# Order statistics in a four-layer graph kernel: z rows by transfers, k and table differences on ScalarE, and the last layers in layer 0's buffers

## The chip, the cores and the metric

The kernel runs on one core of one Trainium2 chip. The metric is the time of one execution on the device in microseconds (us); the kernel before took 14073.2 us (median of three runs, 14069.84 to 14090.67).

## The reference, cut to what matters

There are 16 batch elements of 1024 nodes with 64 channels, and one 1024 x 1024 adjacency matrix each. Four layers follow one another, each of the form `x = x + layer(relu(layernorm(x)), adj)`.

```python
# layer 0: thin the adjacency, then for each node and channel three quantiles over its neighbours
adj_d = _dilate_adj(adj, mask)
sv = jnp.sort(where(valid, x, big)); m = valid.sum(-1)
for tau, wt in zip([.25, .5, .75], [.25, .5, .25]):
    pos = clip(tau * (m - 1), 0); lo = floor(pos); hi = ceil(pos)
    agg += wt * (gather(lo) * (1 - frac) + gather(hi) * frac)
h = relu((x + agg) @ W1 + b1); y = (h @ W2 + b2) * mask
# layer 1: (A + I) x / rowsum        layer 2: attention, 8 heads of 64, softmax(g0*q k^T + g1*adj)
# layer 3: adj @ (x W3) + b3
```

Layer 0 is an order-statistic problem: for each node, channel and six positions k (floor and ceil of three quantiles), the k-th smallest value among the node's neighbours.

## The kernel before, in words

**Layer 0.** The channels of an element are sorted once (`ranks`, a bitonic network on VectorE), and the neighbours are thinned (`dilate`). Then `picks` walks 1536 steps: 16 elements x 8 groups of 8 channels x 2 halves of 512 nodes x 6 positions q. Before the six steps of a (group, half), `group` (L668) counts with matmuls how many neighbours of a node lie below each block of sorted values: `cum` (L694, copied from PSUM by ScalarE) holds the counts, `c0` and `c1` hold packed words. A step then compares `cum` with row `krow[q]` (`le`, L735), masks the two words with it (`wa`, `wb`, L737 and L739), reduces them with matmuls (L751), finds the place within the block (`bits`, L766 to L772) and the value (`value`, L779). After the sixth q of a (group, half), `value` adds the six results (`agg`, L785), weights them (`w`, L794), folds them with the matmul `acc` (L797) into eight rows of a 64-row PSUM tile whose other rows are zero, and VectorE adds (for group 0, copies) all 64 rows to `el.z` (L804, L802). `el.z` is [128, 2, 512]: for each half, 64 rows of h and 64 rows of sums. `leave` (L954) multiplies `z` by W1 twice (`ph`, L962), then by W2, adds to x and gives the element to the later layers.

**What an element needs first.** `stages` (L923) prepares the next element in the last steps of the present one: the neighbour tile, the counts `m1` (L588), six rows `krow` (L602, L603: multiply and add, then shift right, in integers on VectorE; L605: cast to fp16 by ScalarE), and `sorted_table` (L621), whose differences `df` are multiplied out of PSUM by VectorE (L639, four per element). Sorting and thinning of the next element (`background`) are given out one piece per step.

**Layers 1 to 3.** `rest(b)` runs layer 1, layer 2 and layer 3 of an element. The main loop at the end pays it out against the steps: a step is worth 0.42 units, a row block of layer 2 costs 1.0. So the layers of element b run among the steps of element b + 1, and those of the last element run alone after the last step. In layer 2, for each of four pairs of heads (`pr`), k, q and v are made (L1045, L1057), and for each of eight row blocks i: a row block `ad` of the adjacency is loaded (L420, three buffers) and scaled by ScalarE; the scores of two 512-column halves go to one PSUM tile `sp` with one buffer (L1074); VectorE adds `ad` and takes the minimum (L1083); ScalarE takes the exponent of the two heads (`s`, two buffers of tag b4) ; TensorE transposes it through `pcols` (L412), ScalarE copies it to `eT` (L415, two buffers of tag bt), and TensorE multiplies it with v (`ao`, L1093) and the projection (`pp`, L1104).

**What sets the order.** Each engine works its own instructions in one order, fixed when the kernel is built, as does SyncE's queue, from which all transfers are issued. Waits between engines are semaphores. A buffer of a ring (`a2` has four, `b4`, `pa`, `pb`, `pc` two each) is free again when its last reader is done, a transfer included.

**Start.** L130 to L145 make a table of bit-reversed numbers, [128, 1024] with equal rows, by ten rounds of two VectorE operations, and write it to DRAM; `ranks` reads it back (L528) eight times in all.

Of the kernel before, what the change touches and what calls it, by code (L numbers as in the profile page):

```python
# [29 lines left out]
TOP = 2.0 ** 23  # L30
MID = 1600.0
UP = 4096.0
LOW = 2048.0


@with_exitstack
def tile_preln_adj_stack(
# [57 lines left out]
    def a2(name, shape=(P, 512), dt=F32):  # L95
        return sb.tile(list(shape), dt, tag="a2", bufs=4, name=name)
# [5 lines left out]
        return ps.tile(list(shape), dt, tag="pc", bufs=2, name=name)  # L102


    def b4(name, shape=(P, N), dt=F32):
        return sb.tile(list(shape), dt, tag="b4", bufs=2, name=name)

    def pb(name, shape=(P, 512), dt=F32):
        return ps.tile(list(shape), dt, tag="pb", bufs=2, name=name)

    def small(name, shape, dt=F32, bufs=3):
# [6 lines left out]
    def sc(name, shape=(P, P), dt=F32):  # L118
        return scrp.tile(list(shape), dt, name=name)
# [7 lines left out]
    identh = const.tile([P, P], HP, name="identh")  # L127
    nc.vector.tensor_copy(identh, identf)

    rev_i = sc("rev_i", (P, N), I32)  # L130
    nc.gpsimd.iota(rev_i, pattern=[[1, N]], base=0, channel_multiplier=0)
    rev_a = sc("rev_a", (P, N), I32)
    rev_b = sc("rev_b", (P, N), I32)
    nc.vector.memset(rev_a, 0)
    for b_ in range(N.bit_length() - 1):
        up = N.bit_length() - 2 - 2 * b_
# [2 lines left out]
            op1=OP.logical_shift_left if up >= 0 else OP.logical_shift_right,  # L139
        )  # L140
        nc.vector.tensor_tensor(rev_a, rev_a, rev_b, OP.bitwise_or)
    rev = sc("rev", (P, N), HP)
    nc.vector.tensor_copy(rev, rev_a)
    rev_d = dram.tile([P, N], HP, name="rev_d")
    nc.sync.dma_start(rev_d, rev)  # L145
    not_i = const.tile([P, P], BF, name="not_i")
    nc.vector.tensor_scalar(not_i, identf, -1.0, 1.0, op0=OP.mult, op1=OP.add)
# [23 lines left out]
    par = const.tile([P, 2], F32, name="par")  # L171
    nc.vector.tensor_copy(par[:, 1:2], par_i[:, 0:1])
    nc.vector.tensor_scalar(par[:, 0:1], par[:, 1:2], -1.0, 1.0, op0=OP.mult, op1=OP.add)
    for c2 in range(2):
        cols = slice(c2 * BKW, (c2 + 1) * BKW)
        for i, w in enumerate((1.0, LOW)):
            nc.vector.tensor_scalar(
                sel_w[:, i, cols], fcol_i[:, :BKW], 0.0, w, op0=OP.mult, op1=OP.add
            )
            nc.vector.tensor_scalar(sel_w[:, i, cols], sel_w[:, i, cols], par[:, c2 : c2 + 1], None, op0=OP.mult)  # L180
# [44 lines left out]
    for i in range(2):  # L225
        nc.vector.tensor_tensor(sel_t[:, i, 8 * i : 8 * i + 8], pblk[:, 0:8], fcol_i[:, 0:8], OP.is_equal)

    sel_c = const.tile([P, 2 * (D - 8) + 8], F32, name="sel_c")
    nc.vector.memset(sel_c, 0.0)
    nc.vector.tensor_scalar(pblk, prow_i, 7, None, op0=OP.bitwise_and)  # L230
    nc.vector.tensor_tensor(sel_c[:, D - 8 : D], pblk[:, 0:8], fcol_i[:, 0:8], OP.is_equal)


    tab_d = const.tile([P, 2, P], F32, name="tab_d")
# [27 lines left out]
    nc.vector.memset(mid_c[:, 0:1], MID)  # L262
    nc.vector.memset(mid_c[:, 1:2], MID * LOW)
    nc.vector.memset(mid_c[:, 2:3], -MID)

    sel_q = const.tile([P, NQ, 2 * BKW], BF, name="sel_q")
    for q in range(NQ):
# [93 lines left out]
    def act(out_, in_, func=AF.Copy, **kw):  # L361
        nc.scalar.activation(out_, in_, func, **kw)  # L362
# [42 lines left out]

    def chunk_cols(ad, name):

        aT = sb.tile([P, C, P], F32, tag="bt", bufs=2, name=name)
        for s in range(2):
            pt = pb("pcols", (P, 4, P))  # L410
            adjoining(
                nc.tensor.transpose(pt[:, c, :], ad[:, (4 * s + c) * P : (4 * s + c + 1) * P], identf)  # L412
                for c in range(4)
            )
            nc.scalar.copy(aT[:, 4 * s : 4 * s + 4, :], pt)  # L415
        return aT
# [65 lines left out]
    def ranks(V):  # L482
# [42 lines left out]
        nc.sync.dma_start(vs, F)  # L525
        yield "half"
        R = b2_("rev", (P, N), HP)
        nc.sync.dma_start(R, rev_d)  # L528

        last = (len(steps) - 1) // 4  # L530

# [51 lines left out]
    def positions(valid):  # L583

        m1 = sb.tile([P, N], I16, tag="m1", bufs=1, name="m1")  # L588
        for t in range(NH):
            pm = pa("pm")  # L590
            adjoining(
                nc.tensor.matmul(
                    pm, ones, valid[:, j, t * 512 : (t + 1) * 512], start=j == 0, stop=j == C - 1
                )
                for j in range(C)
            )
            nc.vector.tensor_scalar(m1[:, t * 512 : (t + 1) * 512], pm, -1.0, None, op0=OP.add)
        yield None
        krow = []
        for q in range(NQ):  # L600
            n = a2("n", (P, N), I16)
            nc.vector.tensor_scalar(n, m1, q // 2 + 1.0, 3.0 * (q % 2), op0=OP.mult, op1=OP.add)  # L602
            nc.vector.tensor_scalar(n, n, 2, None, op0=OP.logical_shift_right)  # L603
            krow.append(sb.tile([P, N], HP, tag="krow", bufs=NQ, name="krow"))
            nc.scalar.copy(krow[q], n)  # L605
            if q < NQ - 1:
                yield None
        n6 = a2("n6", (P, N), I16)
        nc.vector.tensor_scalar(n6, m1, q_tau, q_add, op0=OP.mult, op1=OP.add)
        nc.vector.tensor_scalar(n6, n6, 2, None, op0=OP.logical_shift_right)  # L610
        kq = sb.tile([P, N], HP, tag="kq", bufs=1, name="kq")
        nc.scalar.copy(kq, n6)
        yield krow, kq
        nr = a2("nr", (P, N), I16)
        nc.vector.tensor_scalar(nr, m1, r_tau, None, op0=OP.mult)
        nc.vector.tensor_scalar(nr, nr, 3, None, op0=OP.bitwise_and)
        coef = sb.tile([P, N], BF, tag="coef", bufs=1, name="coef")
        nc.vector.tensor_scalar(coef, nr, w_frac, w_one, op0=OP.mult, op1=OP.add)
        yield coef

    def sorted_table(s, vs):  # L621

        rows = slice(s * D, (s + 1) * D)
        u = q4("u", (P, 8, D))
        pt = pa("put", (P, 8, D))  # L630
        for q in range(8):
            nc.tensor.transpose(pt[:, q, :], vs[rows, q * P : (q + 1) * P], identf[rows, rows])
        nc.scalar.copy(u, pt)
        df = q4("df", (P, D // 2, 2, 8, 2))
        for e in range(2):
            pd = pa("pd", (P, 8, D // 2, 2))
            nc.tensor.matmul(pd, tab_d[:, e, :], u, start=True, stop=True)
            for c2 in range(2):
                nc.vector.tensor_scalar(  # L639
                    df[:, :, c2, :, e], pd[:, :, :, c2].rearrange("p q c -> p c q"),  # L640
                    par[:, c2 : c2 + 1], UP, op0=OP.mult, op1=OP.mult,
                )
        yield None
        tab = sb.tile([P, 2, D // 2, 2 * BKW], HP, tag="tab", bufs=1, name="tab")
        df = df.rearrange("p c s q e -> p (c s q e)")
        for i in range(2):
            part = tab[:, i].rearrange("p c k -> p (c k)")
            nc.vector.tensor_copy(part, df)
            if i < 1:
                nc.vector.tensor_tensor(df, df, part, OP.subtract)  # L650
        yield tab
# [16 lines left out]
    def group(g, t, bk, pw, valid, weights):  # L668
# [16 lines left out]
        for pp in range(4):  # L685
# [5 lines left out]
                nc.tensor.matmul(pc, cw[:, j, :], valid[:, j, hs], start=j == 0, stop=j == C - 1)  # L691
                for j in range(C)
            )
            nc.scalar.copy(cum[:, pp, :], pc)  # L694
            if late is not None:
                low_part(*late)
            pw_ = pc_("pword")
# [15 lines left out]
    def picks():  # L713
# [61 lines left out]
        def value(n):  # L775
# [5 lines left out]
            if q < NQ - 1:  # L781
# [10 lines left out]
            hs = slice(t * 512, (t + 1) * 512)  # L792
            w = a2("w")
            nc.vector.tensor_tensor(w, agg, el.coef[:, hs], OP.mult)  # L794
            half = slice(t * D, (t + 1) * D)
            acc = pb("acc")
            nc.tensor.matmul(  # L797
                acc[half, :], sel_c[:, D - 8 - 8 * g : 2 * D - 8 - 8 * g], w,
                start=True, stop=True, tile_position=(0, t * D), skip_group_check=True,
            )  # L800
            if g == 0:
                nc.vector.tensor_copy(el.z[half, t, :], acc[half, :])  # L802
            else:
                nc.vector.tensor_tensor(el.z[half, t, :], el.z[half, t, :], acc[half, :], OP.add)  # L804

        els[0] = arrive(0)
        for r in background(0):
# [209 lines left out]
    def layer2(b, xr):  # L1017
# [17 lines left out]
        HW = H * D  # L1035
        for pr in range(H // 2):

            kT = sb.tile([P, N], F32, tag="kT", bufs=1, name="kT")
            qT = sb.tile([P, N], F32, tag="qT", bufs=1, name="qT")
            v = sb.tile([P, C, P], F32, tag="v2", bufs=1, name="v2")  # L1040
            for t in range(NH):
                hs = slice(t * 512, (t + 1) * 512)
                both = ((kT, slice(0, D), pb("pk")), (qT, slice(D, P), pb("pq")))
# [19 lines left out]
            for i in range(C):  # L1063
# [5 lines left out]
                nms = [None, None]  # L1069
                for t in range(NH):  # L1070
                    hs = slice(t * 512, (t + 1) * 512)
                    sps = ps.tile([P, 2, 512], F32, tag="sp", bufs=1, name="sp")
                    adjoining(
                        nc.tensor.matmul(  # L1074
                            sps[:, e, :], qT[e * D : (e + 1) * D, i * P : (i + 1) * P],
                            kT[e * D : (e + 1) * D, hs], start=True, stop=True,
                        )
                        for e in range(2)
                    )
                    for e in range(2):  # L1080

                        nm = small("nm", [P, 1], bufs=6)
                        nc.vector.tensor_tensor_reduce(  # L1083
                            ss[e][:, hs], sps[:, e, :], ad[:, hs], -1.0, 3.0e38 if t == 0 else nms[e],
                            op0=OP.add, op1=OP.min, accum_out=nm,
                        )
                        nms[e] = nm
# [61 lines left out]
    for r in picks():  # L1149
        due += r  # L1150
        while due > 0.0:
            due -= next(two) or due
    for _ in two:
        pass

# [33 lines left out]
```

## Time and profile before

| | |
|---|---|
| median of three runs | 14073.2 us |
| the profiled execution | 14083.12 us |
| its span, first to last instruction | 14080.9 us |
| granted TensorE clock, mean | 0.978 |
| start: until the first compare (L735) | 348 us |
| 1536 steps | 348 to about 13621 us |
| last element's layers 1 to 3 alone | about 13621 to 14081 us |
| VectorE busy | 12849.4 us (91%) |
| TensorE busy (matmuls) | 12452.1 us (88%) |
| ScalarE busy | 8198.1 us (58%) |
| the transfers' share of the 16 DMA engines | 18.8% |

The execution that was profiled took 2.2 us more than its span and 9.9 us more than the median. In a line of the profile, "x" gives how often a group of instructions ran; after the bar stand busy us and the mean ns of one; then the idle time of the engine just ahead of them, and who ended it. A line number can be that of a helper (L362 is the call of every ScalarE activation). GpSimd does next to nothing here.

### The profile page before, as it was taken

How to read it: one execution, taken by the hardware profiler on the slowest of the kernel's cores; microseconds unless marked ns; L12 is line 12 of the kernel's file. 1: busy time of each engine (PE TensorE's matmuls, PEld its weight loads, DVE VectorE, ACT ScalarE, POOL GpSimd, SP SyncE). 2: the span in 40 equal slices, each digit the busy share in tenths (PEclk: the TensorE clock that was granted, in tenths of full speed). 3: DMA queues.
4: the chain of work that ended last, by engine and by line, in shares of the span. 5: the costliest groups of instructions: out<-in, count | busy, mean ns of one | idle time of the engine just before them, and what ended most of it. 6: DMA issues, size and time to landing. Idle time of an engine off the chain costs nothing. (4 is left out here: it accounts for less than half of the span.)

```text
span 14080.9 us, 236134 instructions
## 1 busy us (share of the span) xinstructions
PE 12452.1 (88%) x94402; PEld 5955.5 (42%) x95489; DVE 12849.4 (91%) x23280; ACT 8198.1 (58%) x14170; POOL 25.0 (0%) x138
## 2 busy tenths in 40 slices
PE   1889989999899998999899998998989999999987
PEld 0224444444444444444444444444444444444444
DVE  9999999999999999999999999999989999988863
ACT  1446656566566665656566665665656566665655
POOL 0000000000000000000000000000000000000000
PEclk9999999999999999999999999999999999999999
DMA  3012121211212112121211212122121211202011
GB/s 95 28 35 65 47 82 49 77 55 51 77 47 84 49 55 71 53 79 50 70 57 55 76 49 78 49 66 66 48 76 50 71 61 53 82 25 62 26 58 55
DMA packets 478672, 838.40 MB, mean 60 GB/s; under 512 B 232448, under 2 KB 234624, under 8 KB 477568
## 3 DMA queue, kind: packets, MB, share of 16 engines
q1 hardware_dynamic: 477568, 823.24, 18.8%
q8 instruction: 747, 12.24, 0.4%
q14 instruction: 357, 2.92, 0.1%
HBM read 616.27 MB, written 206.83 MB: 58 GB/s over the span
## 5 line engine op out<-in xcount | busy, mean ns | idle before, releaser
L699 PE MATMUL pword<-valid,dw 128*128 128x512 fp8e4 x8192 | 1985.5, 385 | 141.6 <-DVE dw L665 101.3
L691 PE MATMUL pc<-valid,cw 128*128 128x512 fp8e4 x8192 | 1973.9, 381 | 26.0 <-DVE valid L479 13.9
L737 DVE TENSOR_TENSOR wa<-le,c 128x2048 f16<-128x2048 f16 x1536 | 1865.8, 1215 | 134.8 <-PE prep L751 119.6
L735 DVE TENSOR_TENSOR le<-cum,krow 128x2048 f16<-128x2048 f16 x1536 | 1863.6, 1213 | 16.5 <-PE val L751 16.4
L739 DVE TENSOR_TENSOR wb<-le,c 128x2048 f16<-128x2048 f16 x1536 | 1864.1, 1214 | 3.5 <-PE prep L751 3.3
L362 ACT ACTIVATE s<-s,nm 128x1024 f32<-128x1024 f32 x1024 | 1169.9, 1143 | 728.3 <-DVE nm L1083 727.0
L758 ACT COPY wi<-prep 128x512 f32<-128x512 f32 x1536 | 896.8, 584 | 943.3 <-PE prep L751 796.9
L362 ACT ACTIVATE hi<-pword,mid_c 128x512 f16<-128x512 f32 x1024 | 703.2, 687 | 1140.4 <-PE pword L704 1135.5
L1074 PE MATMUL sp<-kT,qT 64*128 64x512 f32 x4096 | 1168.8, 646 | 200.8 <-DVE nm L1083 192.5
L699 PEld LDWEIGHTS <-dw 128*128 128x128 bf16 x8192 | 763.5, 99 | 1262.6 <-DVE dw L665 228.0
L412 PE MATMUL pcols<-identf,s 128*128 128x128 f32 x8192 | 1156.1, 283 | 155.7 <-ACT s L362 74.7
L691 PEld LDWEIGHTS <-cw 128*128 128x128 bf16 x8192 | 764.5, 98 | 1085.4 <-issue 250.1
L412 PEld LDWEIGHTS pcols<-identf,s 128*128 128x128 f32 x8192 | 913.8, 143 | 627.1 <-ACT eT L415 238.8
L415 ACT COPY eT<-pcols 128x512 f32<-128x512 f32 x2048 | 1110.1, 593 | 85.2 <-PE pcols L412 83.3
L1093 PE MATMUL ao<-eT,v 128*64 128x128 f32 x16384 | 1079.9, 277 | 63.8 <-ACT eT L415 60.7
L751 PE MATMUL val<-le,tab 128*32 128x512 f16 x12288 | 1092.2, 388 | 47.7 <-DVE vs L779 30.4
L779 DVE SCALAR_TENSOR_TENSOR vs<-pz,vs 128x512 f32<-128x512 f32 x1536 | 1045.0, 680 | 65.4 <-PE pv L1057 14.9
L362 ACT ACTIVATE vs<-val 128x512 f32<-128x512 f32 x1536 | 927.1, 604 | 235.7 <-PE val L751 146.3
L1093 PEld LDWEIGHTS ao<-eT,v 128*64 128x64 f32 x16384 | 905.5, 137 | 317.3 <-ACT eT L415 212.6
L694 ACT CAST cum<-pc 128x512 f16<-128x512 f32 x1024 | 603.8, 590 | 719.0 <-PE pc L691 674.7
L751 PE MATMUL prep<-wb,sel_w 128*32 128x512 f16 x6144 | 642.5, 396 | 261.8 <-DVE wb L739 238.5
L362 ACT ACTIVATE c<-pword,mid_c 128x512 f16<-128x512 f32 x1024 | 711.2, 695 | 196.9 <-PE pword L681 182.7
(260 smaller groups left out, 19147.0 us busy)
## 6 DMA issues: line engine op xcount, KB each, us to landing
ad<-in_adj_dram SPq DMA_DIRECT2D x768, 512.0 KB, 3.6
adjT_d<-aT SPq DMA_DIRECT2D x128, 512.0 KB, 4.6
aT<-adjT_d SPq DMA_DIRECT2D x128, 512.0 KB, 3.7
md<-sm SPq DMA_DIRECT2D x216, 256.0 KB, 2.0
sb<-md SPq DMA_DIRECT2D x216, 256.0 KB, 2.9
rem_d<-rem SPq DMA_DIRECT2D x128, 256.0 KB, 2.0
left_d<-left SPq DMA_DIRECT2D x128, 256.0 KB, 2.6
left<-left_d SPq DMA_DIRECT2D x128, 256.0 KB, 3.8
```

Of the source, the lines that this page charges most:

```text
L362: nc.scalar.activation(out_, in_, func, **kw)
L412: nc.tensor.transpose(pt[:, c, :], ad[:, (4 * s + c) * P : (4 * s + c + 1) * P], identf)
L415: nc.scalar.copy(aT[:, 4 * s : 4 * s + 4, :], pt)
L691: nc.tensor.matmul(pc, cw[:, j, :], valid[:, j, hs], start=j == 0, stop=j == C - 1)
L699: nc.tensor.matmul(pw_, dw[:, j, :], valid[:, j, hs], start=j == 0, stop=False, skip_group_check=True)
L735: nc.vector.tensor_tensor(le, cum, bc(el.krow[q][:, None, hs], [P, 4, 512]), OP.is_le)
L737: nc.vector.tensor_tensor(wa, le, c0, OP.mult)
L739: nc.vector.tensor_tensor(wb, le, c1, OP.mult)
L751: nc.tensor.matmul(dst[32 * pp : 32 * pp + 32, :], w[pp], r[pp], start=i in (0, 3), stop=i in (2, 4), tile_position=(0, 32 * pp),)
L779: nc.vector.scalar_tensor_tensor(vs, pz, -191.0, vs, op0=OP.is_equal, op1=OP.mult)
L1074: nc.tensor.matmul(sps[:, e, :], qT[e * D : (e + 1) * D, i * P : (i + 1) * P], kT[e * D : (e + 1) * D, hs], start=True, stop=True,)
L1093: nc.tensor.matmul(ao[e * D : (e + 1) * D, :], v[:, j, e * D : (e + 1) * D], eTs[e][:, j, :], start=j == 0, stop=j == C - 1, tile_position ...
```

## The change

Four things are edited.

1. **Sums into their rows by transfers.** The `acc` matmul gives only the eight rows of its group. ScalarE copies them from PSUM to the first eight rows of `w`, and a transfer of 8 x 512 fp32 (16 KB) puts them into the group's rows of `el.z`. VectorE's copy and adds go.
2. **k and table differences by ScalarE.** A row of `krow` is made by one activation from `m1`: `m1 * (q//2 + 1)/4 + 1032 - 0.375` or `+ 0.375`, whose rounding to fp16 (step 1 above 1024) gives floor or ceil. So that both sides of the compare have the offset, `cum` gets 1032 added, by an activation with a bias in place of a copy. `df` is made by ScalarE with a per-row scale.
3. **The last layers in layer 0's buffers.** When the steps are over, `alone` is set: the `s` tiles come from ring a4 (four buffers), `aT` and `eT` from ring tb (six), PSUM tiles other than `pcols` from ring pa and no longer from pb, every second `sp` from ring pc, and k, q and v of odd head pairs from other tiles.
4. **The bit-reversal table** is made as [128, 8] with the numbers spread over the rows, and read back with a broadcast.

```diff
+BASE = 1032.0
...
+    alone = []
     def b4(name, shape=(P, N), dt=F32):
-        return sb.tile(list(shape), dt, tag="b4", bufs=2, name=name)
+        return a4(name, shape, dt) if alone else sb.tile(list(shape), dt, tag="b4", bufs=2, name=name)
     def pb(name, shape=(P, 512), dt=F32):
+        if alone and name != "pcols":
+            return pa(name, shape, dt)
         return ps.tile(list(shape), dt, tag="pb", bufs=2, name=name)
...
-    rev_i = sc("rev_i", (P, N), I32)
-    nc.gpsimd.iota(rev_i, pattern=[[1, N]], base=0, channel_multiplier=0)
-    rev_a = sc("rev_a", (P, N), I32)
-    rev_b = sc("rev_b", (P, N), I32)
+    rev_i = sc("rev_i", (P, C), I32)
+    nc.gpsimd.iota(rev_i, pattern=[[1, C]], base=0, channel_multiplier=C)
+    rev_a = sc("rev_a", (P, C), I32)
+    rev_b = sc("rev_b", (P, C), I32)
...
-    sel_c = const.tile([P, 2 * (D - 8) + 8], F32, name="sel_c")
+    sel_c = const.tile([P, 8], F32, name="sel_c")
...
+    up_c = const.tile([P, 3], F32, name="up_c")
+    for i, shift in enumerate((-0.375, 0.375, 0.0)):
+        nc.vector.memset(up_c[:, i : i + 1], BASE + shift)
...
-        aT = sb.tile([P, C, P], F32, tag="bt", bufs=2, name=name)
+        aT = (
+            tb(name, (P, C, P), F32) if alone
+            else sb.tile([P, C, P], F32, tag="bt", bufs=2, name=name)
+        )
...
-        nc.sync.dma_start(R, rev_d)
+        nc.sync.dma_start(R, rev_d.rearrange("(o p) c -> o (p c)", o=1).to_broadcast([P, N]))
...
-            n = a2("n", (P, N), I16)
-            nc.vector.tensor_scalar(n, m1, q // 2 + 1.0, 3.0 * (q % 2), op0=OP.mult, op1=OP.add)
-            nc.vector.tensor_scalar(n, n, 2, None, op0=OP.logical_shift_right)
             krow.append(sb.tile([P, N], HP, tag="krow", bufs=NQ, name="krow"))
-            nc.scalar.copy(krow[q], n)
+            act(
+                krow[q], m1, AF.Identity, scale=(q // 2 + 1) / 4.0, bias=up_c[:, q % 2 : q % 2 + 1]
+            )
...
-                nc.vector.tensor_scalar(
-                    df[:, :, c2, :, e], pd[:, :, :, c2].rearrange("p q c -> p c q"),
-                    par[:, c2 : c2 + 1], UP, op0=OP.mult, op1=OP.mult,
+                act(
+                    df[:, :, c2, :, e], pd[:, :, :, c2].rearrange("p q c -> p c q"), AF.Copy,
+                    scale=par_up[:, c2 : c2 + 1],
                 )
...
-            nc.scalar.copy(cum[:, pp, :], pc)
+            act(cum[:, pp, :], pc, AF.Identity, bias=up_c[:, 2:3])
...
-            half = slice(t * D, (t + 1) * D)
-            acc = pb("acc")
-            nc.tensor.matmul(
-                acc[half, :], sel_c[:, D - 8 - 8 * g : 2 * D - 8 - 8 * g], w,
-                start=True, stop=True, tile_position=(0, t * D), skip_group_check=True,
-            )
-            if g == 0:
-                nc.vector.tensor_copy(el.z[half, t, :], acc[half, :])
-            else:
-                nc.vector.tensor_tensor(el.z[half, t, :], el.z[half, t, :], acc[half, :], OP.add)
+            acc = pb("acc", (8, 512))
+            nc.tensor.matmul(acc, sel_c, w, start=True, stop=True)
+            nc.scalar.copy(w[:8, :], acc)
+            nc.sync.dma_start(el.z[t * D + 8 * g : t * D + 8 * g + 8, t, :], w[:8, :])
...
-            kT = sb.tile([P, N], F32, tag="kT", bufs=1, name="kT")
-            qT = sb.tile([P, N], F32, tag="qT", bufs=1, name="qT")
-            v = sb.tile([P, C, P], F32, tag="v2", bufs=1, name="v2")
+            if alone and pr % 2:
+                kT, qT = q4("kT"), q4("qT")
+                v = sb.tile([P, C, P], F32, tag="hT", bufs=1, name="v2")
+            else:
+                kT = sb.tile([P, N], F32, tag="kT", bufs=1, name="kT")
+                qT = sb.tile([P, N], F32, tag="qT", bufs=1, name="qT")
+                v = sb.tile([P, C, P], F32, tag="v2", bufs=1, name="v2")
...
-                    sps = ps.tile([P, 2, 512], F32, tag="sp", bufs=1, name="sp")
+                    if alone and t % 2:
+                        sps = [pc_("sp") for _ in range(2)]
+                    else:
+                        sp = ps.tile([P, 2, 512], F32, tag="sp", bufs=1, name="sp")
+                        sps = [sp[:, e, :] for e in range(2)]
...
+    alone.append(True)
     for _ in two:
         pass
```

More of the change, by code (lines that the diff above doesn't have):

```diff
@@ L141, in tile_preln_adj_stack @@
         nc.vector.tensor_tensor(rev_a, rev_a, rev_b, OP.bitwise_or)
-    rev = sc("rev", (P, N), HP)
+    rev = sc("rev", (P, C), HP)
     nc.vector.tensor_copy(rev, rev_a)
-    rev_d = dram.tile([P, N], HP, name="rev_d")
+    rev_d = dram.tile([P, C], HP, name="rev_d")
     nc.sync.dma_start(rev_d, rev)
@@ L173, in tile_preln_adj_stack @@
     nc.vector.tensor_scalar(par[:, 0:1], par[:, 1:2], -1.0, 1.0, op0=OP.mult, op1=OP.add)
+    par_up = const.tile([P, 2], F32, name="par_up")
+    nc.vector.tensor_scalar(par_up, par, UP, None, op0=OP.mult)
     for c2 in range(2):
@@ L226, in tile_preln_adj_stack @@
         nc.vector.tensor_tensor(sel_t[:, i, 8 * i : 8 * i + 8], pblk[:, 0:8], fcol_i[:, 0:8], OP.is_equal)
-    sel_c = const.tile([P, 2 * (D - 8) + 8], F32, name="sel_c")
-    nc.vector.memset(sel_c, 0.0)
+    sel_c = const.tile([P, 8], F32, name="sel_c")
     nc.vector.tensor_scalar(pblk, prow_i, 7, None, op0=OP.bitwise_and)
-    nc.vector.tensor_tensor(sel_c[:, D - 8 : D], pblk[:, 0:8], fcol_i[:, 0:8], OP.is_equal)
+    nc.vector.tensor_tensor(sel_c, pblk[:, 0:8], fcol_i[:, 0:8], OP.is_equal)
     tab_d = const.tile([P, 2, P], F32, name="tab_d")
@@ L1071, in layer2 @@
                     hs = slice(t * 512, (t + 1) * 512)
-                    sps = ps.tile([P, 2, 512], F32, tag="sp", bufs=1, name="sp")
+                    if alone and t % 2:
[3 more added lines that the diff above has]
+                        sps = [sp[:, e, :] for e in range(2)]
                     adjoining(
                         nc.tensor.matmul(
-                            sps[:, e, :], qT[e * D : (e + 1) * D, i * P : (i + 1) * P],
+                            sps[e], qT[e * D : (e + 1) * D, i * P : (i + 1) * P],
                             kT[e * D : (e + 1) * D, hs], start=True, stop=True,
@@ L1083, in layer2 @@
                         nc.vector.tensor_tensor_reduce(
-                            ss[e][:, hs], sps[:, e, :], ad[:, hs], -1.0, 3.0e38 if t == 0 else nms[e],
+                            ss[e][:, hs], sps[e], ad[:, hs], -1.0, 3.0e38 if t == 0 else nms[e],
                             op0=OP.add, op1=OP.min, accum_out=nm,
```

## The prediction, on record before the run

> **What bounds the kernel now.** I read the page's busy shares first, then the busy time of each engine element by element, then the groups of instructions that the change touches, then what SyncE's queue waits for, and last the timeline of the end.
>
> ```profile
> PE 12452.1 (88%) x94402; PEld 5955.5 (42%) x95489; DVE 12849.4 (91%) x23280; ACT 8198.1 (58%) x14170; POOL 25.0 (0%) x138
> PE   1889989999899998999899998998989999999987
> DVE  9999999999999999999999999999989999988863
> ```
>
> VectorE (DVE) is nearly full up to the last five slices, TensorE (PE) is close behind, ScalarE (ACT) has room. An average can't say which of two nearly full engines decides, so I cut the span by elements (an element begins at its first `le`, L735). In the rows: stretch, its length, busy us (and instructions) of PE, PEld, DVE, ACT, POOL, granted clock, DMA share, GB/s. They are element 0, elements 9, 10, 14, 15 and the end.
>
> ```profile
> 348.00:1068.60 720.60, 581.64 (x3526) 194.67 (x3574) 679.66 (x941) 295.25 (x478) 0.00 (x0) 0.95 0.10 31
> 7783.80:8612.60 828.80, 761.84 (x5902) 367.13 (x5969) 782.82 (x1460) 510.95 (x884) 1.21 (x8) 0.99 0.20 62
> 8612.60:9466.50 853.90, 773.37 (x5919) 371.70 (x5991) 812.97 (x1431) 513.75 (x891) 1.21 (x8) 0.98 0.20 62
> 12002.30:12824.00 821.70, 767.99 (x5893) 368.19 (x5961) 712.63 (x1246) 510.38 (x887) 1.49 (x8) 0.99 0.17 53
> 12824.00:13621.00 797.00, 743.21 (x5701) 353.56 (x5770) 643.88 (x1091) 475.23 (x839) 1.49 (x8) 0.99 0.12 38
> 13621.00:14080.90 459.90, 342.51 (x2619) 229.16 (x2616) 150.91 (x484) 240.27 (x430) 1.06 (x7) 0.87 0.23 73
> ```
>
> Elements 1 to 14 take (12824.0 - 1068.6)/14 = 839.7 us on average, in pairs: even ones near 850 with 812 us of VectorE work, odd ones near 833 with 783. Element 14, which has no sorting beside it, has 71 us less VectorE work than an odd one, with TensorE's work nearly unchanged, and is only 11 us shorter. So from 812 to 783 a us off VectorE brought 0.6 us, and below 783 only 0.16: at about 54 us above TensorE's own 768 a second bound stands. What the change takes off VectorE will not come back whole.
>
> **What VectorE loses.** The groups, and on ScalarE the nearest rows for what is new:
>
> ```profile
> L804 DVE TENSOR_TENSOR z<-z,acc 64x512 f32<-64x512 f32 x224 | 153.1, 683 | 111.7 <-PE acc L797 109.5
> L802 DVE COPY z<-acc 64x512 f32<-64x512 f32 x32 | 22.0, 687 | 14.3 <-PE acc L797 14.1
> L603 DVE TENSOR_SCALAR n<-n 128x1024 int16<-128x1024 int16 x96 | 39.8, 416 | 0.0
> L639 DVE TENSOR_SCALAR df<-pd,par 128x256 f32<-128x256 f32 x64 | 27.3, 474 | 2.5 <-PE pd L637 2.2
> L694 ACT CAST cum<-pc 128x512 f16<-128x512 f32 x1024 | 603.8, 590 | 719.0 <-PE pc L691 674.7
> L362 ACT ACTIVATE hi<-pword,mid_c 128x512 f16<-128x512 f32 x1024 | 703.2, 687 | 1140.4 <-PE pword L704 1135.5
> L362 ACT ACTIVATE cumn<-cumn,sk 128x1024 f16<-128x1024 f16 x128 | 146.8, 1147 | 137.0 <-DVE sk L450 126.8 <-DVE sk L451 10.0
> ```
>
> z: 153.1 + 22.0 busy and 111.7 + 14.3 idle, in which VectorE stood for `acc` with all its later work behind it: 301 us, 18.8 per element. k rows: L603 and its twin L602, 79.6 us, 5.0 per element, in the crowded last steps of an element. Differences: 29.8 us, 1.9 per element. Together 25.7 per element; neighbouring VectorE instructions overlap by about 0.07 us, which takes 2 off: 23.5 us.
>
> What comes of it:
> - Element 0 has VectorE at 94% and TensorE idle for 139 us: I take 20.
> - Elements 1 to 14: an even one 0.6 x 23.5 = 14, an odd one between 0.16 and 0.6 of it, 4 to 14, I take 10 because 7.9 of the 23.5 are a stall that nothing else filled. Mean 12, sum 168. Bounds: 4 each (56) if TensorE's bound is met at once, 23.5 each (329) if VectorE decides all the way.
> - Element 15: TensorE is busy 93%, VectorE 81%; 5 (0 to 19).
> - Start: ten pairs of VectorE operations on 128x1024 integers (0.68 and 1.21 us), a memset 0.91, a cast 0.68: 20.5 us, less the overlap 18. With eight columns each costs about as a 128x8 row does (0.16): 22 x 0.16 = 3.5. Saved 15. Element 0's own k rows and differences lie here too: 5. Sum 20 (15 to 24).
>
> **What is added.** ScalarE gets 1024 x 0.097 = 99 us for `cum` (687 against 590), 96 x 0.10 = 10 for k rows (1147 against 1045), 64 differences of 128x256, between the 128x128 copy (0.27) and the 128x512 activation (0.69), say 0.45: 29 us, and 256 copies of 8x512, by the row's length 0.585 each: 150 us. That is 288 us, 18 per element, on an engine with 318 us free in an element of 829. TensorE waited for `cum` 33 times in all, so 0.1 us later is some 3 us. ScalarE's copy now waits for `acc` as VectorE did, with `wi` and `vs` of the next step queued behind it; ScalarE mostly waits for TensorE there anyhow. Cost 0 to 30, I take 3. `acc` itself still streams 512 fp32 columns: unchanged.
>
> [...]
>
> **The 256 transfers.** Rows for small and nearby transfers (KB each, median us to landing), and SyncE's queue:
>
> ```profile
> mk_u<-in_nodemask_dram SPq DMA_DIRECT2D x1, 16.0 KB, 1.7
> md<-sm SPq DMA_DIRECT2D x216, 256.0 KB, 2.0
> SPq L420 <- DVE nm L1083: 5554.6, 478, 47.4
> ```
>
> [...] Per element the last transfer is on the path: `acc` 0.6, copy 0.6, transfer 2.0, where before an add of 0.7 stood; in the built order `ph` stands a few us of other matmuls behind `acc`. TensorE, with the next step's `prep` queued behind `ph`, loses 0 to 2.5 us, I take 0.5: 8 us.
> The queue is the other place. Each transfer waits on SyncE for ScalarE's copy; behind it stand the `ad` loads, which ScalarE waits for, and the sort's stores. Now the queue mostly waits for an `ad` buffer to come free (5554.6 us): it runs ahead, and every transfer takes that lead away until it is issued. Also the fourth a2 tile after `w`, a `wi` or `bit` two steps on, waits until the transfer has landed; two steps are 17 us, the chain is 4. I take 4 us (0 to 60). With ScalarE's 3: 15 us for all that is added.
>
> **The end.** One row block of layer 2 takes half of 17.6 us now:
>
> ```profile
> 13861.65 1.13 PE L1074 MATMUL sp<-kT,qT 64*128 64x512 f32 x4
> 13864.51 1.13 PE L1074 MATMUL sp<-kT,qT 64*128 64x512 f32 x4 [1.31 <-DVE nm L1083]
> 13868.89 1.13 PE L1074 MATMUL sp<-kT,qT 64*128 64x512 f32 x4 [0.79 <-DVE nm L1083]
> 13869.95 1.97 PE L1093 MATMUL ao<-eT,v 128*64 128x128 f32 x32
> 13873.50 0.49 PE L1104 MATMUL pp<-wproj,aoT 128*128 128x128 f32 x2 [1.58 <-ACT aoT L1102]
> ```
>
> TensorE stands for the minimum (one `sp` buffer) and for `aoT`. Its own work per block is 2 x 1.1 `sp`, 2 x 1.1 `pcols`, 1.9 `ao`, 0.4 `pp` = 6.7 us, ScalarE's 5.9. With second buffers the built order has the exponents of the next block ahead of this block's copies, so 6.7 is the floor, 8.8 (no gain) the other end; I take 7.4, near the floor: 32 x 1.4 = 45. Layer 1's eight blocks take 3.3 us with 2.5 us of matmuls: 5. Layer 3 and the norms are the same, and the order at the head of a head pair (`pk` after the last `pp`) is too. Sum 50 (20 to 70).
>
> **Sum.** 20 + 20 + 168 + 5 + 50 - 15 = 248 us. Against the profiled execution: 14083.1 - 248 = 13835; the median of the runs is 9.9 lower, so 13825.
>
> **Rivals.**
> - *TensorE's bound takes the steps* (20%). For it: element 14's small gain. Against it: the even elements, and TensorE's waits for `wb`, `bit` and `dw`. Then 56 in the body, 35 at start and element 0, 35 at the end, less 25: 13970.
> - *VectorE decides throughout* (12%). For it: 95% busy. Then 329 + 40 + 5 + 65 less 5: 13640.
> - *Slower: SyncE's queue holds up the loads* (5%). Every z transfer keeps the `ad` loads behind it until ScalarE has copied, and ScalarE's scaling then waits for a load of 3.6 us. At 2.0 us on the path for each, 512 - 263 = 249 lost: 14320. It turns the sign from 263/256 = 1.03 us per transfer. Against it: 608 stores (of `rem`, `left`, `sm` and `aT`) wait in that queue in the same way now, and ScalarE's waits for `ad` sum to 89.5 us only.
> - *Hardly a change* (3%): VectorE's freed time turns wholly into waits for TensorE and the end doesn't shorten.
>
> The forecast has 60%. Under 0.2% (28 us) a measurement can't tell a change. Range: from halfway to the second case up to the first one, 13690 to 13970.
>
> **What would show it.** Right: VectorE about 350 us less busy, `wa` waiting longer for `prep`; odd and even elements closer together, near 828; the end near 410 us; landing of z transfers near 2 us and no long wait of `ph`. Wrong: `ad` waits of ScalarE above 200 us, `ph` standing 3 us and more, or elements still at 840.

## The result, and the profile after

| | before | changed | forecast |
|---|---|---|---|
| median, us | 14075.3 (4 runs) | 13945.2 (4 runs, 13938.1 to 13956.7) | 13825 (13690 to 13970) |
| ratio, 95% interval | | 0.9908 [0.9892, 0.9924] | 0.982 |
| span of the profiled execution, us | 14080.9 | 13954.9 | |
| start, to the first compare | 348 | 324 | -20 |
| element 0 | 721 | 711 | -20 |
| elements 1 to 14 | 11755 | 11720 | -168 |
| element 15 | 797 | 802 | -5 |
| the last layers alone | 460 | 398 | -50 |
| granted TensorE clock, mean | 0.978 | 0.978 | |

The change saves 130 us and not 248. The time is inside the range, close to its upper end, where the rival "TensorE's bound takes the steps" (13970) had been put. (The forecasts of the stages do not yet hold the 15 us that I charged for all that is added.) Elements 1 to 14 take 837.1 us on average and took 839.7: "elements still at 840" was a sign that the prediction had named for being wrong.

The busy shares of the changed kernel, as on its page:

```profile
PE 12582.4 (90%) x95489; PEld 5956.5 (43%) x95489; DVE 12588.9 (90%) x22771; ACT 8441.5 (60%) x14490; POOL 24.4 (0%) x138
```

VectorE did 260.5 us less work, and its idle time grew from 1231.5 to 1366.0 us: of 260 us, 134 came back as standing. The same stretches as ahead of the prediction (start, elements 0, 9, 10, 14, 15, and the end):

```profile
0.00:323.90 323.90, 39.43 (x172) 18.20 (x173) 294.77 (x738) 41.95 (x53) 1.50 (x11) 0.99 0.34 103
323.90:1034.80 710.90, 594.26 (x3572) 195.10 (x3572) 666.72 (x919) 311.34 (x498) 0.00 (x0) 0.93 0.10 32
7735.40:8568.20 832.80, 771.98 (x5981) 365.72 (x5980) 768.76 (x1431) 526.33 (x904) 1.49 (x8) 0.99 0.20 62
8568.20:9405.90 837.70, 772.53 (x5970) 367.71 (x5963) 793.37 (x1389) 524.94 (x907) 1.21 (x8) 0.98 0.20 64
11918.70:12754.30 835.60, 783.83 (x5962) 369.97 (x5962) 697.80 (x1216) 526.24 (x904) 1.55 (x8) 0.98 0.17 53
12754.30:13556.70 802.40, 750.67 (x5804) 353.19 (x5802) 632.65 (x1072) 490.40 (x859) 1.49 (x8) 0.99 0.12 38
13556.70:13954.90 398.20, 342.82 (x2624) 233.09 (x2616) 151.27 (x484) 236.60 (x431) 1.06 (x7) 0.88 0.26 84
```

Element 9 has 14 us less on VectorE than before and takes 4 us more; element 10 has 20 less and takes 16 less; element 14 has 15 less and takes 14 more. The saving follows no element's VectorE work. Over all, cut in the same way, the even elements 2 to 12 went from 850.3 to 848.8 us, the odd ones 1 to 13 from 833.1 to 827.3, and element 14 from 821.7 to 835.6. The forecast had the most for the even ones; they gained the least, and even and odd ones lie further apart than before.

What ScalarE took over:

```profile
L373 ACT ACTIVATE cum<-pc,up_c 128x512 f16<-128x512 f32 x1024 | 707.6, 691 | 700.5 <-PE pc L705 669.2 <-DVE le L749 15.9 <-DVE bit L780 4.9
...
L811 ACT COPY w<-acc 8x512 f32<-8x512 f32 x256 | 145.7, 569 | 187.1 <-PE acc L810 186.4 <-PE val L765 0.7
...
L373 ACT ACTIVATE krow<-m,up_c 128x1024 f16<-128x1024 int16 x96 | 109.8, 1154 | 20.1 <-DVE le L749 16.2 <-DVE m L611 3.6
...
L373 ACT ACTIVATE df<-pd,par_up 128x256 f32<-128x256 f32 x64 | 27.0, 498 | 2.3 <-PE pd L651 2.3
```

The first three means lie within 3% of my estimates (687, 585, 1147 ns); the table differences take 498 ns and not 450, 3 us in all. SyncE's queue (first the wait for an `ad` buffer, then the z transfers waiting for ScalarE's copy):

```profile
SPq L434 <- DVE nm L1099: 4319.6, 474, 46.7
SPq L812 <- ACT w L811: 1604.0, 166, 29.7
```

By this row the queue stands 1604 us at the copies, and its wait for `ad` buffers, which is its lead, shrinks by 1235 us (5554.6 to 4319.6). Yet ScalarE waits for `ad` for 86.0 us in all, against 89.5: the lead was large enough. When a z transfer lands isn't in the trace.

### The profile page after: what moved, and what is told of

It is laid out like the page before. It is cut to its first block, busy times and chain, and to the rows that moved or that the text cites. A ratio compares the mean times of both kernels' runs of the same rounds, so it can differ in the third digit from the quotient of the medians.

```text
span 13954.9 us, 237846 instructions
## 1 busy us (share of the span) xinstructions
PE 12582.4 (90%) x95489; PEld 5956.5 (43%) x95489; DVE 12588.9 (90%) x22771; ACT 8441.5 (60%) x14490; POOL 24.4 (0%) x138
## 5 line engine op out<-in xcount | busy, mean ns | idle before, releaser
L765 PE MATMUL val<-le,tab 128*32 128x512 f16 x12288 | 1136.1, 388 | 52.4 <-DVE vs L793 34.2
L793 DVE SCALAR_TENSOR_TENSOR vs<-pz,vs 128x512 f32<-128x512 f32 x1536 | 1050.1, 684 | 123.4 <-PE pz L786 96.9
L1109 PE MATMUL ao<-eT,v 128*64 128x128 f32 x16384 | 1121.5, 278 | 42.1 <-ACT eT L429 38.2
L373 ACT ACTIVATE cum<-pc,up_c 128x512 f16<-128x512 f32 x1024 | 707.6, 691 | 700.5 <-PE pc L705 669.2
L1099 DVE CUSTOM_DVE_ANT_0 s<-sp,ad,nm 128x512 f32<-128x512 f32 x1024 | 730.2, 746 | 88.9 <-PE sp L1090 88.3
```

Source lines behind the costliest of these rows:

```text
L765: nc.tensor.matmul(dst[32 * pp : 32 * pp + 32, :], w[pp], r[pp], start=i in (0, 3), stop=i in (2, 4), tile_position=(0, 32 * pp),)
L793: nc.vector.scalar_tensor_tensor(vs, pz, -191.0, vs, op0=OP.is_equal, op1=OP.mult)
L1109: nc.tensor.matmul(ao[e * D : (e + 1) * D, :], v[:, j, e * D : (e + 1) * D], eTs[e][:, j, :], start=j == 0, stop=j == C - 1, tile_position ...
```

## The experiments

The parts are called END (edit 3), KS (edit 2), SUMS (edit 1) and REV (edit 4). **My theory** after the result: in the steps both VectorE and TensorE are nearly full and wait for each other, so time taken off VectorE comes back as waits for TensorE. **Rivals:** the sums cost what they save (the transfers in SyncE's queue, or the `a2` tile that each holds until it has landed); or TensorE alone bounds the steps. A third came up on the way: the built order of the instructions shifts with every edit, and its luck is as large as what I try to measure. Before ran beside every group of experiments, at a median of 14073.7 to 14078.2 us.

### e1_end_only: END alone

```diff
+        if alone and name != "pcols":
+            return pa(name, shape, dt)
...
+    alone.append(True)
```

> The kernel before with the edits of the end alone (buffers of layer 0 for the last element's layers). Both theories: the steps stay as they were, the end falls from 460 to about 398 us, so about 14013 us in all (-62). If the reordering of the end costs elsewhere, less.

Measured: 14018.1 us, ratio 0.9962 [0.9947, 0.9977]. The end takes 397 us, the steps 11757 (before: 11755; their built order is the same, so this is also a repeat). So the end's whole saving is END, and it's there without the rest. Blocks of layer 2 in the changed kernel, TensorE's timeline:

```profile
13806.81 1.96 PE L1109 MATMUL ao<-eT,v 128*64 128x128 f32 x30 [0.48 <-ACT eT L429]
13808.70 1.09 PE L426 MATMUL pcols<-identf,s 128*128 128x128 f32 x8
13809.79 0.49 PE L1120 MATMUL pp<-wproj,aoT 128*128 128x128 f32 x2
13810.21 1.13 PE L1090 MATMUL sp<-kT,qT 64*128 64x512 f32 x4
13811.27 1.09 PE L426 MATMUL pcols<-identf,s 128*128 128x128 f32 x8
13812.29 0.43 PE L1109 MATMUL ao<-eT,v 128*64 128x128 f32 x2
13812.65 1.13 PE L1090 MATMUL sp<-kT,qT 64*128 64x512 f32 x4
13813.71 1.96 PE L1109 MATMUL ao<-eT,v 128*64 128x128 f32 x30
...
13817.24 0.49 PE L1120 MATMUL pp<-wproj,aoT 128*128 128x128 f32 x2 [0.55 <-ACT aoT L1118]
```

From `pp` to `pp` are 7.45 us, and so it stays for the middle blocks of a head pair; I had put 7.4. One stall of about 0.5 is left in a block, at `eT` or `aoT`, and the waits for `nm` are gone from these blocks.

This run also shows a fault in what I had read. Its steps are those of before, but its trace has all matmuls. The count for `pz<-wi`, in e1 and then in before:

```profile
L779 PE MATMUL pz<-wi,less_k 128*128 128x512 bf16 x1536 | 601.9, 392 | 0.0
```
```profile
L772 PE MATMUL pz<-wi,less_k 128*128 128x512 bf16 x455 | 180.5, 397 | 0.4 <-issue 0.2
```

1081 of 1536 records are missing in before's trace. Elements 9, 10 and 14 in e1:

```profile
7787.20:8615.20 828.00, 770.25 (x5970) 367.18 (x5969) 782.89 (x1461) 511.48 (x884) 1.22 (x8) 0.99 0.20 62
8615.20:9464.10 848.90, 775.74 (x5992) 367.85 (x5991) 812.59 (x1431) 513.89 (x891) 1.22 (x8) 0.99 0.20 62
12007.90:12828.70 820.80, 775.66 (x5963) 367.26 (x5961) 712.76 (x1247) 510.66 (x887) 1.49 (x8) 0.99 0.17 53
```

TensorE is busy 770, 776 and 776 us, where before's trace gave 762, 773 and 768. Element 14's bound stands 45 us above TensorE's work, not 54. The hint was on before's page: matmuls x94402, weight loads x95489.

### e2_sums_only: SUMS alone

```diff
+            acc = pb("acc", (8, 512))
+            nc.tensor.matmul(acc, sel_c, w, start=True, stop=True)
+            nc.scalar.copy(w[:8, :], acc)
+            nc.sync.dma_start(el.z[t * D + 8 * g : t * D + 8 * g + 8, t, :], w[:8, :])
```

> The kernel before with the sums put in their rows by transfers, nothing else. VectorE loses 18.8 us per element, ScalarE gains 256 copies, SyncE 256 transfers. Theory 'TensorE's bound' (what VectorE gives up is worth little since TensorE has no more to give): between 14015 and 14075. Theory 'added work takes it back' (VectorE's time is worth 0.5 us per us, and ScalarE's copies and the transfers cost some 9 us per element): also little here, 14000 to 14075, but then the run without the adds and without the transfers must be 100 us and more faster than this one. If this one is slower than before (over 14090), the transfers cost more than the adds.

Measured: 14086.1 us, ratio 1.0008 [0.9999, 1.0017]. The most expensive thing taken off VectorE, 301 us by its row with the standing, gave nothing: steps 11786 us, 31 more than before.

### e3_k_only: KS alone

```diff
+            act(
+                krow[q], m1, AF.Identity, scale=(q // 2 + 1) / 4.0, bias=up_c[:, q % 2 : q % 2 + 1]
+            )
...
+            act(cum[:, pp, :], pc, AF.Identity, bias=up_c[:, 2:3])
```

> The kernel before with k rows and table differences by ScalarE and the bias on the counts, nothing else. VectorE loses 6.9 us per element, ScalarE gains 0.1 us on each of 1024 count copies. TensorE's bound: 14040 to 14075. VectorE's time worth half: about 14020. If the later counts hurt TensorE: above 14075.

Measured: 14041.5 us, ratio 0.9977 [0.9968, 0.9986]. 33 us saved: 8 at the start, 41 in elements 1 to 14, the rest given back in element 0 and the end.

### e4_no_adds, e5_sums_other_ring, e6_sums_pool_queue, e7_sums_no_transfers: what the sums cost

Four edits around SUMS. e4 is the kernel before without its adds; e5 is e2 with the copy in a tile that lives longer anyhow; e6 is e2 with the transfers on GpSimd's queue; e7 is e2 without transfers.

```diff
 # e4, against before
-            else:
-                nc.vector.tensor_tensor(el.z[half, t, :], el.z[half, t, :], acc[half, :], OP.add)
 # e5, against e2
-            nc.scalar.copy(w[:8, :], acc)
+            nc.scalar.copy(vs[:8, :], acc)
...
 # e6, against e2
-            nc.sync.dma_start(el.z[t * D + 8 * g : t * D + 8 * g + 8, t, :], w[:8, :])
+            nc.gpsimd.dma_start(el.z[t * D + 8 * g : t * D + 8 * g + 8, t, :], w[:8, :])
 # e7, against e2
-            nc.sync.dma_start(el.z[t * D + 8 * g : t * D + 8 * g + 8, t, :], w[:8, :])
+            if g == 0:
+                half = slice(t * D, (t + 1) * D)
+                nc.vector.tensor_copy(el.z[half, t, :], vs[half, :])
```

> The kernel before without VectorE's 224 adds to z (the sums of groups 1 to 7 are left out of the output); the copies of group 0 stay, nothing is put in their place. VectorE loses 153 us of work and 112 us of standing for the matmul. TensorE's bound: the steps gain 40 us or less, so 14035 and above. Added work takes it back: VectorE's relief alone brings 0.5 us per us, 130 us, so about 13945.

Measured: 14007.9 us, ratio 0.9953 [0.9938, 0.9967]: 67 us for 153.1 us of adds and 111.7 us of standing before them, about half of the 130 that 0.5 us per us would have given.

> As the run with the sums alone (14086), but ScalarE copies the eight rows into the last value tile vs (a ring of eight, one taken per step), so that the transfer no longer holds a tile of ring a2. If the held ring is what cost the sums their gain: 14008 to 14050. If not: 14075 to 14095.

Measured: 14036.8 us, ratio 0.9973 [0.9964, 0.9983]: 49 us faster than e2.

> As the run with the sums alone (14086), but the 256 transfers are issued from GpSimd's queue, which has nothing else to do. If they cost by holding up the loads and stores behind them in SyncE's queue: 14008 to 14050. If not: 14075 to 14095.

Measured: 14086.0 us, ratio 1.0005 [0.9996, 1.0014]: the same as e2 to 0.1 us. SyncE's wait for `ad` buffers in e6 is back where it was in before (5554.6):

```profile
SPq L419 <- DVE nm L1076: 5571.6, 481, 45.4
```

So the queue did get its lead back, and it was worth nothing. The rival "SyncE's queue holds up the loads" falls.

> As the run with the sums alone (14086), with ScalarE's copies but without any transfer (the sums are left out of the output; for group 0 VectorE copies 64 rows as in the kernel before, so VectorE's work is that of the run without adds, 14008). If ScalarE's copies cost the 78 us between those two: near 14086. If the transfers cost them, by the queue, the ring or the wait at the end of an element: near 14008.

Measured: 14052.4 us, ratio 0.9979 [0.9972, 0.9987]: 34 below e2 and 45 above e4. It lies between both expectations and settles nothing by itself, for a reason that e11 shows.

### e8_less_matmul: less work for TensorE

```diff
-                for i in range(2)
+                for i in range(1)
...
```

> The kernel before without the second round of table matmuls (four of 20 per step; the low half of the table values is left out of the output): 0.27 us per step off TensorE, 415 us in all, nothing else changed. If TensorE is the bound of the steps: 250 to 400 us less, 13675 to 13825. If VectorE is: 20 to 120 less, 13955 to 14055.

Measured: 13927.7 us, ratio 0.9895 [0.9879, 0.9912]: 151 us less than before on the same chip. By the row of `val` the cut is worth 373 us of TensorE (1098.5 in e1, 725.6 here), by the page's sum 265 (12452.1 to 12187.1, both traces with some 1,000 matmul records missing): 0.40 to 0.57 us per us. That is more than if TensorE had slack, and less than if it were the bound. But e8 also ran at a lower granted clock, 0.971 against 0.978; on its page the two slices that hold most of element 0 stand at 8 tenths of full speed where before's stand at 9, and element 1 begins at 1081.0 us against 1068.6. The 33 executions of before beside this group go from 14062 us at 0.980 to 14101 at 0.976, and a line through them gives 8.5 us per 0.001. By that (an estimate) the lower clock cost e8 about 60 us, and TensorE's work is worth more than the 151 say. VectorE's wait `wa` for `prep` falls from 119.6 to 74.1 us.

### e9_all_other_ring: the changed kernel with e5's edit

```diff
-            nc.scalar.copy(w[:8, :], acc)
-            nc.sync.dma_start(el.z[t * D + 8 * g : t * D + 8 * g + 8, t, :], w[:8, :])
+            nc.scalar.copy(vs[:8, :], acc)
+            nc.sync.dma_start(el.z[t * D + 8 * g : t * D + 8 * g + 8, t, :], vs[:8, :])
```

> The changed kernel (13945) with the eight rows copied into vs and not into w, so that no transfer holds a tile of ring a2. If the held ring costs in the whole change what it cost alone (50 us): 13895, between 13875 and 13920. If it doesn't add up, 13945.

Measured: 13912.3 us (13907.7 to 13915.4), ratio 0.9886 [0.9871, 0.9901]. It beats both kernels, the changed one by 33 us; the two kernels' runs don't overlap.

### e10_all_but_sums: END, KS and REV, with VectorE's adds kept

```diff
-            acc = pb("acc", (8, 512))
-            nc.tensor.matmul(acc, sel_c, w, start=True, stop=True)
-            nc.scalar.copy(w[:8, :], acc)
-            nc.sync.dma_start(el.z[t * D + 8 * g : t * D + 8 * g + 8, t, :], w[:8, :])
+            acc = pb("acc")
...
+                nc.vector.tensor_tensor(el.z[half, t, :], el.z[half, t, :], acc[half, :], OP.add)
```

> The changed kernel with VectorE's adds to z kept as before (k rows, differences, end and start changed). If the sums by transfers bring nothing, as alone (+11): 13925 to 13950, level with the changed kernel. If they pay once the other parts are in: 13970 to 14020.

Measured: 13957.1 us, ratio 0.9923 [0.9906, 0.9939]. 12 us above the changed kernel, with overlapping intervals. The sums by transfers, the first edit named in the change, have no gain that these runs can show (e10's own runs go from 13935 to 13976). The other three add up: END 57, KS 33, and REV 16 (start 339.6 us in e3, 323.3 here, no run of its own) make 106 of e10's 117.

### e11_other_pace: a control

Before, with the value of a step in layer units changed by 0.24%. No work is added or removed; pieces of the later layers fall between other steps, and a few that stood in the end fall into the steps.

```diff
-            yield .42
+            yield .421
```

> A control: the kernel before with the layers paid out at 0.421 units per step and not 0.42; no work is added or left out, only the interleaving moves a little. It says how far a shift of the built order alone moves the steps of elements 1 to 14 (11755 us in the kernel before). If by less than 15 us, differences of 30 us and more between the parts are those of the parts. If by 30 us and more, a part of what the runs show is the order's luck.

Measured: 13991.4 us, ratio 0.9943 [0.9928, 0.9958]: 82 us less, with the same work. In the profiled execution 62 us fall in elements 1 to 14. Cut at the last `vs`, element 15 takes 785 us against 799 and the end 438 against 458, with a row block each of layer 2 and layer 3 fewer in it. e11's granted clock was 0.979 to 0.981, before's beside it 0.978 to 0.979; at the rate given for e8 that stands for some 20 us, and whether the order brought the better clock isn't shown. Elements 1 to 14 in e11, in e1 and in the changed kernel:

```profile
1071.00:12764.10 11693.10, 10694.26 (x82459) 5142.19 (x83425) 11054.31 (x20029) 7159.65 (x12386) 23.60 (x112) 0.99 0.19 62
```
```profile
1072.10:12828.70 11756.60, 10863.54 (x83361) 5157.79 (x83360) 11056.34 (x20013) 7153.84 (x12377) 20.19 (x112) 0.98 0.19 61
```
```profile
1034.80:12754.30 11719.50, 10855.20 (x83330) 5156.88 (x83328) 10843.52 (x19566) 7361.23 (x12652) 20.36 (x112) 0.98 0.20 62
```

With VectorE's work the same to 2 us (11054 and 11056), e11 is 63 us shorter than e1, and 26 shorter than the changed kernel, which has 211 us less. This sets the scale for all of the above:

| elements 1 to 14, us | length | VectorE busy |
|---|---|---|
| before | 11755 | 11055 |
| e1 | 11757 | 11056 |
| e11 | 11693 | 11054 |
| e3 | 11714 | 10983 |
| e10 | 11690 | 10980 |
| e4 | 11688 | 10934 |
| e7 | 11742 | 10930 |
| e2 | 11786 | 10925 |
| e5 | 11724 | 10920 |
| e6 | 11766 | 10920 |
| changed | 11720 | 10844 |
| e9 | 11678 | 10843 |

Each row is one execution; e10's was the fastest of its four, 22 us below its median. A straight line through these twelve has a slope of 0.08 us per us (standard error 0.15, correlation 0.17), and the lengths scatter by 35 us (standard deviation). The forecast's 168 us for 213 us of VectorE's work would be a slope of 0.8. So that is out, while one of 0.3 is not. And no part's effect in the steps of 70 us or less (KS, the ring of the copies, the adds of e4) is shown apart from the order's luck. For the ring two pairs have one sign (e2 to e5 -49, changed to e9 -33): likely, not shown.

### e12_both_less: e8 and e4 together

```diff
-                for i in range(2)
+                for i in range(1)
...
-            else:
-                nc.vector.tensor_tensor(el.z[half, t, :], el.z[half, t, :], acc[half, :], OP.add)
```

> The kernel before with both reliefs at once: no adds to z by VectorE (alone 67 us less) and no second round of table matmuls (alone 150 us less); both leave out a part of the output as said there. If one engine after the other is the bound, in turns, relief of both frees more than the sum: 300 us and more less, 13775 or below. If what is left is the chains of single steps (waits of any engine for any other), the two add up: 217 less, about 13860.

Measured: 13809.4 us, ratio 0.9812 [0.9798, 0.9827]: 264 us below before, the single gains being 67 and 151; it lies between both expectations. Elements 1 to 14 of e8, then of e12:

```profile
1081.00:12700.30 11619.30, 10504.98 (x77031) 5066.68 (x77951) 11043.09 (x20008) 7121.94 (x12375) 19.26 (x112) 0.98 0.19 62
```
```profile
1063.90:12583.60 11519.70, 10462.44 (x77029) 5049.21 (x77950) 10919.50 (x19817) 7121.39 (x12375) 18.71 (x112) 0.98 0.19 62
```

These two leave the scatter of the table: 136 and 236 us below before. With TensorE relieved, the same adds are worth 100 us in the steps instead of 67. That fits two engines that wait for each other, but the difference of 33 is within the scatter.

## Why the prediction was half right

**The end: right.** Forecast 50, measured 62, and e1 puts it on END. The middle blocks take 7.45 us, as estimated. What came on top lies at the ends of a head pair: in the first three pairs the last two blocks are done in 9 us where they took 17 to 19, and from the last `pp` of a pair to the first of the next are 19.3 us where there were 21 to 22, which I had called unchanged. Against that, the 5 us expected of layer 1 didn't come: from the last step to the first `pk` are 91 us in both kernels.

**The start: right.** Forecast 20, measured 24: by the starts of e3 and e10, 8 for KS and 16 for REV, where I had 5 and 15.

**What is added: in part.** SyncE's queue isn't the transfers' price (e6), and the slower rival is refuted. For `ph`'s later rows I had 8 us. TensorE's idle time just before `ph` is 7.6 us in all in the changed kernel and was 7.4, so no such wait shows. VectorE's wait for what follows (`o` for `y`) did grow from 17.0 to 43.7 us, but it's 36.4 in e4 and 31.3 in e7, which have no transfers; it isn't their price. ScalarE's copies were put too low: VectorE's `vs` (L793) stood 20.8 us behind them, where I took 3. For the ring I took 4, and the two pairs with e5's edit say 33 to 49, not shown apart from the order.

**The step that failed: elements 1 to 14, "an even one 0.6 x 23.5 = 14", 168 in sum, measured 36.** The slope of 0.6 came from comparing even and odd elements of one trace. These differ in more than VectorE's work: TensorE has 5 us more to do in the even one, and the pieces of the other layers fall elsewhere. e11 shows that where they fall alone moves the steps by 62 us. The even elements, by this slope the best place for the saving, gained 1.6 us each and not 14. Moreover 7.9 of the 23.5 us per element were standing for `acc`; with `acc` gone VectorE stands for the next thing. VectorE's waits over the whole run in e1 (whose steps are before's), then in the changed kernel:

```profile
DVE xr L1121 <- PE pp L1119: 200.5, 124, 5.1
DVE s L1098 <- PE sp L1089: 133.5, 120, 13.2
DVE wa L744 <- PE prep L758: 117.6, 86, 5.2
DVE z L811 <- PE acc L804: 108.4, 117, 2.4
...
DVE w L801 <- PE agg L792: 76.2, 64, 9.1
...
DVE vs L786 <- PE pz L779: 62.0, 63, 5.7
```
```profile
DVE xr L1122 <- PE pp L1120: 239.1, 145, 5.1
DVE s L1099 <- PE sp L1090: 179.3, 134, 13.2
DVE wa L751 <- PE prep L765: 170.3, 110, 5.8
DVE w L808 <- PE agg L799: 103.6, 72, 8.9
DVE vs L793 <- PE pz L786: 96.9, 75, 7.8
...
DVE o L978 <- PE y L974: 43.7, 15, 9.2
DVE le L749 <- PE val L765: 36.1, 25, 3.2
DVE eq L676 <- PE pz L785: 29.5, 14, 4.4
```

`acc` is gone with its 108 us, but `xr`, `s`, `wa`, `w` and `vs` wait 39, 46, 53, 27 and 35 us longer. This isn't the luck of one order. The three waits `xr`, `s` and `wa` add up to 429 to 465 us in the five runs that keep the adds (before, e1, e3, e10 and the control e11), and to 560 to 609 in the seven without them (e2, e4 to e7, e9 and the changed kernel). The standing for `acc`, 126 us in before, has moved on to other results of TensorE. In sum, from e1 to the changed kernel, elements 1 to 14: 212.8 us less work on VectorE, 175.7 us more idle time (700.3 to 876.0), 37.1 us gained. How large the gain would be in another order isn't known; that the whole time came to lie in the range is in part luck, since a shift like e11's could have put it outside or near 13880.

I had expected "VectorE about 350 us less busy"; it's 260. In the 350 I had counted the 126 us of standing for `acc` as work. The rows of the removed work sum to 302 with the start, less 32 for overlap: 270. The lower end of the range is a slip too: halfway to 13640 is 13732 and not 13690. Nothing turned on it.

**The rivals.** "TensorE's bound takes the steps" (13970) came nearest in time, and its 56 for the body is near the measured 36. But as a mechanism it isn't shown: if TensorE were the bound, e8's 265 to 373 us would have come back nearly whole, and 151 did, or some 210 if the estimate for its lower clock holds. So it is weakened and not refuted. Had before's trace had all its matmuls, TensorE would have stood at 770 to 776 us per element instead of 762 to 773, and I would have weighed this case higher. "VectorE decides throughout" is refuted by e2 and the table.

**What stays open:** whether holding an `a2` tile until a transfer lands is what SUMS lost in the steps, or the order alone; for that, each variant would have to run at several paces, which wasn't tried.

## What to carry to other kernels

Here two engines were both near 90% (VectorE 91%, TensorE 88%), and work taken off one mostly turned into waits: 213 us off VectorE in elements 1 to 14 gave 37, with 176 us more idle time; two unlike elements of one trace were no measure of what a us is worth. The 126 us that VectorE stood for `acc` were not saved with the instruction that stood; ask what an engine will stand for next. Where the order is fixed at build time, first run a control that changes the order and no work; here 0.24% of pace moved the time by 82 us (0.6%), 62 of them in the steps, and the largest of the four edits gave 57. Compare the number of matmuls with the number of weight loads (94402 and 95489 in before, 95489 of each in the changed kernel) before judging which engine has room.

## What the runs showed of the hardware

- **The fixed order repeated; another order of the same work differed by more.** The steps of before and e1, one execution each, agree within 2 us in 11,755; those of e11 differ by 62. Whole executions of before spread by 39 us (33 of them), and the longer ones have the lower granted clock: 14062 us at 0.980, 14101 at 0.976.
- **The clock of layer 3 at the end.** After a pause of TensorE of 6.4 us the last layer runs at a granted clock of 0.50 to the end of the kernel, in before (from 14046.9 us on) and in the changed kernel (from 13920.8 on) alike; in the 9 us ahead of the pause it is 1.00 in both. The last 25 us of the changed kernel:

```profile
13930.00:13954.90 24.90, 18.24 (x127) 14.53 (x126) 1.77 (x8) 1.86 (x7) 0.00 (x0) 0.50 0.43 137
```

A group of 16 matmuls `two` takes 1.98 us there and 1.09 at a clock of 1.00 (the group at 1935.6 us). With TensorE busy for 18.2 us of the 21.2 up to its last matmul, and a stall of 0.42 in every block, the clock stays at 0.50. After an equal pause earlier in the same trace (6.39 us, to 13571.6) it is 0.50 too, from 13571.6 to 13579.9 us, with TensorE busy for 8.27 of these 8.30 us, and 1.00 from there to 13592.0. Whether the stalls are what holds the clock at 0.50 in the last layer isn't shown: no experiment kept TensorE busy over that pause, so what it would bring wasn't tried.
